# Gate logits of a graph-network stage as row sums on VectorE instead of narrow matmuls on TensorE

## The chip, the cores and the metric

The kernel runs on one core of a Trainium2 chip. The metric is the device time of one execution in microseconds (us), lower is better. Engines are called PE (TensorE matmul; PEld is its weight load), DVE (VectorE), ACT (ScalarE), POOL (GpSimd) and SP (SyncE, here a queue that issues DMAs). Lines such as L1123 are lines of the kernel before.

## The reference

A graph has 10000 nodes with 512 features (D) and 160000 edges, sorted by their target `dst`. Two layers follow each other. The first is a mixture of four experts of two graph convolutions each, the second a graph transformer. What the change touches is the first layer:

```
def gnn_layer(x, gate_W, gate_b, Wl, bl, Wr, edge_index):
    gates = softmax(x @ gate_W + gate_b)             # 10000 x 4
    top_v, top_i = top_k(gates, 2)
    inv_deg = 1 / max(deg, 1)  (0 where deg is 0)
    for e in range(4):                               # the experts
        h = x
        for l in range(2):
            aggr = segment_sum(h[src], dst) * inv_deg
            h = relu(aggr @ Wl[e, l] + bl[e, l] + h @ Wr[e, l])
    out = the two chosen experts' h, weighted by top_v, summed
x = layernorm(x + gnn_layer(x, ...))
...
x = layernorm(x + transformer_layer(x, ...))
```

The gate logits are the product `x @ gate_W`, with gate_W of 512 x 4, plus a bias of four numbers.

## The kernel before

The nodes are cut into 79 blocks of 128. The first stage (about the first 4.2 ms) computes the first convolution of all four experts, the second the second convolution, and the last the transformer layer. The change touches only the first stage.

**The first stage** goes over 40 superblocks of two blocks (the first one has a single block). For a block, the features of the edges' sources are fetched by indirect DMAs of POOL (`pull`, L1059) into a ring of ten tiles and summed by target with one-hot matmuls (`p_ag`, L1084); the one-hot tile `oh` and its sums `slots` are made on DVE (L891, L1070), and a small matmul with ones (L1092) gives the degree, from which DVE makes `inv_deg` (L1095). ACT scales the sum to `ag`. `turned_all` transposes `ag` and the block's own rows `xb` on PE (L1107) and ACT copies both into one tile `tt`. The gate logits are then matmuls of `tt`'s transposed `xb` (four weights of 128x128 per block) by `gw`, of 4 columns (L1182), and DVE adds the bias into `gate_w` (L1184). `conv` for one expert is 64 matmuls of 128x128 by 128x256 and ReLU on ACT (L1123, L1125); `products` multiplies the result by the second layer's Wl (L1133), copies to `y` and stores `y_tab` and `h_tab` by SP's queue.

The gather of the next superblock is cut in five pieces, called drives here (each two rounds of four matmuls per block column, 16 records on PE), and they are put between the other work. The order on PE per superblock is: drive 1, gates, conv 0, drive 2, conv 1, drive 3, prod 0, conv 2, drive 4, prod 1, conv 3, drive 5, prod 2, transposes of the next superblock, prod 3. The order on PE, DVE, ACT and POOL is the order in which the program is written (a manual schedule); SP's order is set by a scheduler.

**Work alongside.** Between the parts of `conv` the function `side` issues steps of another job, the ordering of the edges by source for the transformer layer. Until about 1.45 ms these are steps of `plan_src` on DVE: 158 counts (L913, four per call of `side`), then prefix sums in which PE multiplies by the tile `upper` (L930, L937; `upper` is made by an iota on POOL and a comparison on DVE, L927), then 158 scans of three instructions (L947, L950, L951). After that, `side` issues `scatter_src`: seven indirect DMAs of POOL (L993) per `conv`.

**Scratch.** The plan's tiles `m`, `num_i`, `dig_i`, `upper` and `part` are tiles of their own, and `h` has four buffers, one for each expert.

Of the kernel before, what the change touches and what calls it, by code (L numbers as in the profile page):

```python
# [8 lines left out]
F32 = mybir.dt.float32  # L9
BF16 = mybir.dt.bfloat16  # L10
I32 = mybir.dt.int32
U8 = mybir.dt.uint8
AF = mybir.ActivationFunctionType
ALU = mybir.AluOpType
# [616 lines left out]
def fast(ctx: ExitStack, tc: tile.TileContext, a: dict, out: bass.AP, bad: bass.AP):  # L631
# [240 lines left out]
    for e in range(NE):  # L872
        load_to(wl[e], a["L0_gnn_Wl"][e, 0])
        load_to(wr[e], a["L0_gnn_Wr"][e, 0], nc.scalar)
    gw = load_w(wp, "gw", a["L0_gnn_gate_W"], KD, NE)
    gb = wp.tile([P, NE], F32, name="gb")
    nc.sync.dma_start(gb, rows_bcast(a["L0_gnn_gate_b"], NE))
    bl = wp.tile([P, NE, KD], F32, name="bl")
# [17 lines left out]
    DIG = 1024.0  # L896
    SC = max(C, 2 * D)

    def plan_src(pool, ps):
        src_i = pool.tile([P, SC], I32, name="scan")[:, :C]  # L900
        nc.sync.dma_start(src_i, a["src"].rearrange("(p c) -> p c", c=C))
        pair = pool.tile([P, SC], BF16, name="pair")[:, :C]
        digit = pool.tile([P, C], BF16, name="digit")
        nc.vector.tensor_single_scalar(addr_i, src_i, 6, op=ALU.logical_shift_right)
        nc.vector.tensor_copy(pair, addr_i)
        nc.vector.tensor_scalar(addr_i, src_i, 5, 1, op0=ALU.logical_shift_right,
                                op1=ALU.bitwise_and)
        nc.vector.tensor_scalar(digit, addr_i, DIG - 1.0, 1.0, op0=ALU.mult, op1=ALU.add)
        yield
        count = pool.tile([P, NPR], F32, name="count")  # L910
        for b in range(NPR):
            m = pool.tile([P, C], BF16, name="m")
            nc.vector.scalar_tensor_tensor(m, pair, float(b), digit, op0=ALU.is_equal,  # L913
                                           op1=ALU.mult, accum_out=count[:, b:b + 1])
            yield
        num_i = pool.tile([P, NPR], I32, name="num_i")
        dig_i = pool.tile([P, NPR], I32, name="dig_i")
        nc.vector.tensor_copy(num_i, count)
        num = pool.tile([P, NPR, 2], F32, name="num")
        nc.vector.tensor_single_scalar(dig_i, num_i, 1023, op=ALU.bitwise_and)  # L920
        nc.vector.tensor_copy(num[:, :, 0], dig_i)
        nc.vector.tensor_single_scalar(dig_i, num_i, 10, op=ALU.logical_shift_right)
        nc.vector.tensor_copy(num[:, :, 1], dig_i)
        upper = pool.tile([P, P], F32, name="upper")
        nc.gpsimd.iota(upper, pattern=[[1, P]], base=0, channel_multiplier=-1,
                       allow_small_or_imprecise_dtypes=True)
        nc.vector.tensor_scalar(upper, upper, 0.0, None, op0=ALU.is_gt)  # L927
        flat = num.rearrange("p b q -> p (b q)")
        total = ps.tile([P, 512], F32, name="mm")
        nc.tensor.matmul(total[:, :NW], ones, flat, start=True, stop=True)  # L930
        top = pool.tile([P, 2], F32, name="top")
        nc.vector.tensor_reduce(top[:, 0:1], total[:, :NW], axis=AX.X, op=ALU.max)
        nc.vector.tensor_reduce(top[:, 1:2], total[:, :NW], axis=AX.X, op=ALU.add)
        nc.vector.tensor_scalar(fail[:, 1:2], top[:, 0:1], float(SL), None, op0=ALU.is_gt)
        nc.vector.tensor_scalar(fail[:, 2:3], top[:, 1:2], float(E), None, op0=ALU.not_equal)
        first = ps.tile([P, 512], F32, name="mm")
        nc.tensor.matmul(first[:, :NW], upper, flat, start=True, stop=True)  # L937
        two = first[:, :NW].rearrange("p (b q) -> p b q", q=2)
        nc.vector.tensor_copy(num, two)
        nc.vector.scalar_tensor_tensor(count, num[:, :, 1], DIG, num[:, :, 0],  # L940
                                       op0=ALU.mult, op1=ALU.add)
        nc.vector.memset(addr, 0.0)
        yield
        one = ones[:, 0:1].to_broadcast([P, C])
        for b in range(NPR):
            m = pool.tile([P, C], BF16, name="m")
            nc.vector.scalar_tensor_tensor(m, pair, float(b), digit, op0=ALU.is_equal,  # L947
                                           op1=ALU.mult)
            s = pool.tile([P, SC], F32, name="scan")[:, :C]
            nc.vector.tensor_tensor_scan(s, one, m, count[:, b:b + 1], op0=ALU.mult, op1=ALU.add)  # L950
            nc.vector.copy_predicated(addr, m.bitcast(mybir.dt.int16), s)  # L951
            yield

        nc.vector.tensor_sub(addr, addr, digit)
        rank = pool.tile([P, SC], I32, name="scan")[:, :C]
        nc.vector.tensor_copy(rank, addr)
        nc.vector.tensor_scalar(digit, digit, 1.0, 10.0 / (DIG - 1.0), op0=ALU.subtract,
                                op1=ALU.mult)
        nc.vector.tensor_copy(addr_i, digit)
        nc.vector.tensor_tensor(rank, rank, addr_i, op=ALU.logical_shift_right)  # L960
        yield
        nc.vector.tensor_scalar(digit, digit, 0.1, None, op0=ALU.mult)
        nc.vector.scalar_tensor_tensor(addr, pair, 2.0, digit, op0=ALU.mult, op1=ALU.add)
        nc.vector.tensor_scalar(addr, addr, float(CAP), None, op0=ALU.mult)
        part = pool.tile([P, C], I32, name="part")
        nc.vector.tensor_scalar(part, rank, 7, 7, op0=ALU.logical_shift_right,
                                op1=ALU.bitwise_and)
        nc.vector.tensor_add(addr, addr, part)
        nc.vector.tensor_single_scalar(part, rank, P - 1, op=ALU.bitwise_and)
        nc.vector.scalar_tensor_tensor(addr_i, part, float(NC), addr, op0=ALU.mult, op1=ALU.add)  # L970
        yield
# [75 lines left out]
    with p1, tc.tile_pool(name="p1k", bufs=1) as kp, tc.tile_pool(name="p1", bufs=2) as dp, \  # L1047
# [62 lines left out]
        def turned_all(rows):  # L1110
            tt = dp.tile([P, 2, KD, 2 * P], F32, name="tt", bufs=1)
            for i, (b, xb, ag) in enumerate(rows):
                turned(ag, tt[:, 0, :, i * P:(i + 1) * P])
                turned(xb, tt[:, 1, :, i * P:(i + 1) * P])
            return tt

        def conv(tt, e, n):
            h = dp.tile([P, KD, 2 * P], F32, name="h", bufs=4)
            for f in range(KD):
                ph = pm.tile([P, D], F32, name="mm")  # L1120
                for i, w in enumerate((wl[e], wr[e])):
# [17 lines left out]
            nc.sync.dma_start(h_tab[s, :, e, :, :n], h[:, :, :n])  # L1139

        fill = fill_slots()
        plan = plan_src(kp, pm)
        scat = scatter_src(mp)
        planned, planning = [], [0]

# [19 lines left out]
        with tc.manual_schedule(engines={ET.PE, ET.DVE, ET.Activation, ET.Pool}):  # L1165
# [7 lines left out]
            for s in range(NSB):  # L1173
# [2 lines left out]
                more = gather(s + 1, ahead) if s + 1 < NSB else iter(())  # L1176

                drive(more, 1)
                for i, (b, xb, ag) in enumerate(rows):
                    pg = psm.tile([P, NE], F32, name="small")  # L1180
                    for k in range(KD):
                        nc.tensor.matmul(pg, tt[:, 1, k, i * P:(i + 1) * P], gw[:, k, :],  # L1182
                                         start=(k == 0), stop=(k == KD - 1))
                    nc.vector.tensor_add(gate_w[:, b, :], pg, gb)  # L1184
                h = []
                for e in range(NE):
                    h.append(conv(tt, e, n))
# [614 lines left out]
```

## Time and profile before

| What | Value |
|---|---|
| Time before, median of 4 runs | 11294.47 us (11210.12 to 11340.56) |
| Profiled execution, own time | 11198.82 us |
| Its span | 11197.0 us |
| Mean granted clock of PE | 0.957 |
| First stage | to about 4200 us |
| PE, DVE, ACT, POOL busy | 9895.5, 5398.5, 2941.7, 7054.4 us |
| Largest group on PE | conv, L1123: 8960 matmuls, 2003.4 us |

Times are in microseconds, and mean durations of one instruction in nanoseconds. A line of the groups reads: line, engine, operation, output and inputs, shapes, number; then busy time and mean of one; then the idle time of the engine just before them, and what ended it. "issue" is idle time in which no wait is seen. A matmul of f32 appears as two records (two passes), so 16 records in a line are 8 matmuls.

### The profile page before, as it was taken

The page shows a single profiled execution, that of the slowest core. Times are in us where ns is not written, and L with a number is a line of the kernel's source. Part 1 is how long each engine was busy: PE and PEld are TensorE (multiplying, and loading weights), DVE is VectorE, ACT ScalarE, POOL GpSimd, SP SyncE. Part 2 cuts the span into 40 slices and gives each one's busy share as a digit, 9 for nine tenths or more (in the row PEclk, how much of TensorE's full clock was granted, in tenths as well). Part 3 has the DMA queues.
Part 4 walks back from the last instruction along what each step waited for, and adds up shares of the span by engine and source line. Part 5 has one row for each costly group of instructions (what it writes and reads, how often), then busy time and mean ns, then how long its engine had stood idle before and what let it go on. Part 6 is the DMA issues. An engine that isn't in the chain of part 4 may idle for free.

```text
span 11197.0 us, 169204 instructions
## 1 busy us (share of the span) xinstructions
PE 9895.5 (88%) x63887; PEld 5680.3 (51%) x63887; DVE 5398.5 (48%) x8205; ACT 2941.7 (26%) x5390; POOL 7054.4 (63%) x6972
## 2 busy tenths in 40 slices
PE   7999999999999988888888989888788888888887
PEld 4666666656666654333333333333555555555554
DVE  6888930000000022333333333334888888788886
ACT  1111111111111111111111111111455555555554
POOL 5566666666666655665666656665666666666664
PEclk8999999999999989999999999998899999999999
DMA  6554554444444436777777777776777777777774
GB/s 200 180 158 154 157 159 145 144 133 144 147 145 150 149 96 232 239 263 237 252 244 261 251 233 262 247 244 212 231 226 235 226 227 235 221 227 226 226 223 129
DMA packets 1110443, 2258.69 MB, mean 202 GB/s; under 512 B 284587, under 2 KB 534342, under 8 KB 1108848
## 3 DMA queue, kind: packets, MB, share of 16 engines
q0 software_dynamic: 622352, 1654.70, 46.4%
q1 hardware_dynamic: 479546, 579.42, 15.7%
q10 hardware_dynamic: 7718, 13.65, 0.4%
q8 instruction: 507, 8.31, 0.3%
q14 instruction: 320, 2.62, 0.1%
HBM read 2300.44 MB, written 380.18 MB: 239 GB/s over the span
## 4 chain that ended last, share of the span: by engine, by line
PE 70%; DVE 10%; ACT 7%; issue 7%; another core or an unknown queue 4%; DMA 1%; POOL 0%; SPq 0%; ACTq 0%; DVEq 0%; POOLq 0%
PE mm L1123 18%; PE mm L1133 9%; PE mm L1314 8%; PE mm L1276 7%; PE p_ag L1353 6%; PE p_ag L1084 4%; PE bank L1542 3%; PE sums L1632 3%; PE bank L1551 3%; PE bank L1502 2%; DVE m L913 2%; PE qe L1690 2%; DVE s L1731 2%; ACT L1544 2%
## 5 line engine op out<-in xcount | busy, mean ns | idle before, releaser
L1059 POOL DMA_INDIRECT ring<-in_x_dram,idx_t x1580 | 1917.2, 1213 | 1240.9 <-PE p_ag L1084 719.8
L1123 PE MATMUL mm<-tt,big 128*128 128x256 f32 (+1 forms) x8960 | 2003.4, 381 | 41.6 <-issue 39.9
L1123 PEld LDWEIGHTS mm<-tt,big 128*128 128x128 f32 x8960 | 1696.9, 192 | 360.4 <-issue 124.2
L993 POOL DMA_INDIRECT sorted<-pay,addr x1250 | 1263.2, 1011 | 385.5 <-issue 364.8
L1476 POOL DMA_INDIRECT kv<-kv_all,meta x1185 | 1284.6, 1084 | 332.3 <-issue 227.2
L1314 PE MATMUL mm<-big,hb 128*128 128x512 f32 x2528 | 1210.5, 613 | 102.2 <-issue 94.3
L1259 POOL DMA_INDIRECT y<-y_tab,ix x920 | 935.3, 1017 | 478.6 <-issue 216.9
L1276 PE MATMUL mm<-big,z_t 128*128 128x512 f32 x1896 | 923.4, 625 | 262.5 <-DVE t L1321 209.8
L1133 PE MATMUL mm<-wn,h 128*128 128x512 f32 x2528 | 1128.5, 599 | 1.6 <-issue 1.4
L1259 POOL DMA_INDIRECT ring<-y_tab,ix x660 | 679.2, 1029 | 637.2 <-PE p_ag L1353 365.0
L891 DVE TENSOR_TENSOR oh<-loc_t,iota_w 128x640 f32<-128x640 bf16 x158 | 130.8, 829 | 1780.0 <-remote 652.4
L1125 ACT ACTIVATE h<-mm,bl 128x256 f32<-128x256 f32 (+1 forms) x640 | 297.1, 471 | 2533.6 <-PE mm L1123 1356.2
L1542 PE MATMUL bank<-big,big 128*128 128x256 f32 (+1 forms) x2560 | 673.1, 406 | 221.4 <-ACT big L1544 212.8
L1314 PEld LDWEIGHTS mm<-big,hb 128*128 128x128 f32 x2528 | 480.4, 195 | 734.5 <-issue 687.0
L1704 DVE TENSOR_TENSOR kv<-qe,kv 128x1024 f32<-128x1024 f32 x711 | 729.4, 1040 | 159.1 <-PE qe L1690 158.2
L1133 PEld LDWEIGHTS mm<-wn,h 128*128 128x128 f32 x2528 | 469.0, 191 | 602.2 <-issue 581.3
L1618 POOL TENSOR_TENSOR ohp<-oh,p 128x512 f32<-128x512 bf16 x316 | 331.1, 1048 | 688.5 <-ACT p L1609 687.0
L1276 PEld LDWEIGHTS mm<-big,z_t 128*128 128x128 f32 x1896 | 374.2, 200 | 752.5 <-issue 502.1
L1377 ACT ACTIVATE t<-t,gsel 128x512 f32<-128x512 f32 x158 | 109.2, 723 | 2328.4 <-DVE t L1375 1552.4
L1542 PEld LDWEIGHTS bank<-big,big 128*128 128x128 f32 x2560 | 496.7, 203 | 384.5 <-ACT big L1544 272.0
L1731 DVE TENSOR_REDUCE s<-kv 128x40 f32<-128x2560 f32 x237 | 663.8, 2801 | 0.0
L1551 PE MATMUL bank<-big,big 128*128 128x512 f32 x1264 | 595.4, 597 | 57.0 <-ACT big L1544 56.2
(251 smaller groups left out, 14138.4 us busy)
## 6 DMA issues: line engine op xcount, KB each, us to landing
y_tab<-y SPq DMA_DIRECT2D x632, 256.0 KB
hb<-h_tab SPq DMA_DIRECT2D x316, 256.0 KB
h_tab<-h SPq DMA_DIRECT2D x156, 512.0 KB
kv_all<-kvt SPq DMA_DIRECT2D x79, 516.0 KB
xb<-in_x_dram SPq DMA_DIRECT2D x156, 256.0 KB
q_all<-q SPq DMA_DIRECT2D x79, 384.0 KB
q<-q_all SPq DMA_DIRECT2D x237, 128.0 KB
ring<-in_x_dram,idx_t POOLq DMA_INDIRECT x1580
```

The lines of the kernel that those rows point to most:

```text
L993: inst = nc.gpsimd.indirect_dma_start(out=sorted1[:], out_offset=bass.IndirectOffsetOnAxis(ap=addr_i[:, c0 + c:c0 + c + 1], axis=0), in_=p ...
L1059: nc.gpsimd.indirect_dma_start(out=gbuf[i % GB], out_offset=None, in_=x, in_offset=bass.IndirectOffsetOnAxis(ap=window(idx_t, b)[:, j, c:c ...
L1123: nc.tensor.matmul(ph[:, :n], w[:, k, f * P:(f + 1) * P], tt[:, i, k, :n], start=(i + k == 0), stop=(i == 1 and k == KD - 1))
L1133: nc.tensor.matmul(py, h[:, k, i * P:(i + 1) * P], wn[e][:, k, :], start=(k == 0), stop=(k == KD - 1))
L1259: nc.gpsimd.indirect_dma_start(out=ybuf[i % YB], out_offset=None, in_=y_flat, in_offset=bass.IndirectOffsetOnAxis(ap=ahead[b][1][:, j, c:c ...
L1276: nc.tensor.matmul(po, z_t[:, k, :], wqkv[i][:, k, :], start=(k == 0), stop=False)
L1314: nc.tensor.matmul(pr, hb[:, k, :], wr[e][:, k, :], start=(k == 0), stop=False)
L1476: nc.gpsimd.indirect_dma_start(out=kvb[w % KB][:, c, :], out_offset=None, in_=kv_all[:], in_offset=bass.IndirectOffsetOnAxis(ap=blocks[b][ ...
L1542: nc.tensor.matmul(ph, up(f, k), z_t[:, k, :m], start=(k == 0), stop=(k == KD - 1))
L1551: nc.tensor.matmul(po, hid[:, k, i * P:(i + 1) * P], w2[k // KD][:, k % KD, :], start=(k == 0), stop=False)
L1704: nc.vector.tensor_tensor(k, qe.pop((w, g))[:, :len(cs), :], k, op=ALU.mult)
L1731: nc.vector.tensor_reduce(s, kv[:, :, :D].rearrange("p c (h d) -> p c h d", h=H), axis=AX.X, op=ALU.add)
```

## The change

The matmuls of L1182 and the add from PSUM go. In `turned_all`, after a block's transposes, DVE multiplies the block's untransposed rows `xb` by one column of the gate weights, four times, and the instruction's accumulator gives the row sum directly to `gate_w`; a fifth instruction adds the bias. The gate weights are for that laid on all 128 partitions as a tile of 512 x 4 (8 KB per partition), with the four experts side by side, so that one expert's column has a stride of 16 bytes. The products themselves are written to a tile that nobody reads (`unread`, bf16).

To make room, `h` has three buffers instead of four, and one tile `part` is shared by `m`, `num_i`, `dig_i`, `upper`, `part` and `unread`.

```diff
-    gw = load_w(wp, "gw", a["L0_gnn_gate_W"], KD, NE)
+    gw = wp.tile([P, D, NE], F32, name="gw")
+    gate_wt = a["L0_gnn_gate_W"]
+    nc.sync.dma_start(gw, bass.AP(tensor=gate_wt.tensor, offset=gate_wt.offset,
+                                  ap=[[0, P], [1, D * NE]]))
...
-    def plan_src(pool, ps):
+    def plan_src(pool, ps, part):
...
-            m = pool.tile([P, C], BF16, name="m")
+            m = part.bitcast(BF16)[:, :C]
...
-        num_i = pool.tile([P, NPR], I32, name="num_i")
-        dig_i = pool.tile([P, NPR], I32, name="dig_i")
+        num_i, dig_i = part[:, P:P + NPR], part[:, P + NPR:P + 2 * NPR]
...
-        upper = pool.tile([P, P], F32, name="upper")
+        upper = part.bitcast(F32)[:, :P]
...
-        part = pool.tile([P, C], I32, name="part")
+        part = part[:, :C]
...
             for i, (b, xb, ag) in enumerate(rows):
                 turned(ag, tt[:, 0, :, i * P:(i + 1) * P])
                 turned(xb, tt[:, 1, :, i * P:(i + 1) * P])
+                for e in range(NE):
+                    nc.vector.scalar_tensor_tensor(unread, xb, 1.0, gw[:, :, e], op0=ALU.mult,
+                                                   op1=ALU.mult, accum_out=gate_w[:, b, e:e + 1])
+                nc.vector.tensor_add(gate_w[:, b, :], gate_w[:, b, :], gb)
             return tt
 
         def conv(tt, e, n):
-            h = dp.tile([P, KD, 2 * P], F32, name="h", bufs=4)
+            h = dp.tile([P, KD, 2 * P], F32, name="h", bufs=3)
...
-        plan = plan_src(kp, pm)
+        part = kp.tile([P, SC], I32, name="part")
+        unread = part.bitcast(BF16)[:, SC:SC + D]
+        plan = plan_src(kp, pm, part)
...
                 drive(more, 1)
-                for i, (b, xb, ag) in enumerate(rows):
-                    pg = psm.tile([P, NE], F32, name="small")
-                    for k in range(KD):
-                        nc.tensor.matmul(pg, tt[:, 1, k, i * P:(i + 1) * P], gw[:, k, :],
-                                         start=(k == 0), stop=(k == KD - 1))
-                    nc.vector.tensor_add(gate_w[:, b, :], pg, gb)
                 h = []
```

More of the change, by code (lines that the diff above doesn't have):

```diff
@@ L945, in plan_src @@
         for b in range(NPR):
-            m = pool.tile([P, C], BF16, name="m")
+            m = part.bitcast(BF16)[:, :C]
             nc.vector.scalar_tensor_tensor(m, pair, float(b), digit, op0=ALU.is_equal,
```

## The prediction

> **What bounds the kernel now.** I read the 40 slices of the span first, because the diff touches one stage only, and then the chain that ended last.
>
> ```profile
> PE   7999999999999988888888989888788888888887
> DVE  6888930000000022333333333334888888788886
> ...
> PE 70%; DVE 10%; ACT 7%; issue 7%; another core or an unknown queue 4%; DMA 1%; POOL 0%; SPq 0%; ACTq 0%; DVEq 0%; POOLq 0%
> ```
>
> Each digit stands for 280 us. The first stage fills the first fifteen. In slices 2 to 5 both engines are nearly full: DVE works off the plan of the sorted edges (counts L913, then scans L947 to L951). From slice 6 to 14 DVE has almost nothing to do and PE still shows 9. So moving work from PE to DVE meets a full engine first and an empty one later. The view by windows gives the two parts in numbers (columns: stretch, length, then busy time of PE, PEld, DVE, ACT, POOL, the granted clock, DMA share, GB/s).
>
> ```profile
> 398.00:1469.00 1071.00, 1071.00 (x4805) 731.00 (x4797) 961.31 (x633) 172.05 (x331) 720.10 (x441) 1.00 0.50 157
> 1567.00:4042.00 2475.00, 2376.72 (x10028) 1559.62 (x10028) 156.36 (x372) 354.59 (x691) 1605.50 (x1684) 0.98 0.47 145
> ```
>
> In the first stretch PE is busy all the time, 97.2 us per superblock of two blocks (eleven in 1071 us), and DVE 961 / 11 = 87.4 us of them. In the second a superblock takes mostly 105.0 us and 107.6 in the mean (23 in 2475 us), although PE has the same work: some 8 us go to stalls. The PE timeline of one superblock shows the larger one (start, length, instruction, number; in brackets idle time and its releaser), and POOL's timeline stands beneath it.
>
> ```profile
> 1775.19 1.92 PE L1084 MATMUL p_ag<-ring,oh 128*32 128x512 f32 x16
> 1777.05 1.95 PE L1182 MATMUL small<-gw,tt 128*128 128x4 f32 x16
> 1778.85 14.06 PE L1123 MATMUL mm<-tt,big 128*128 128x256 f32 x64
> 1792.84 1.06 PE L1084 MATMUL p_ag<-ring,oh 128*32 128x512 f32 x6
> 1794.22 1.02 PE L1084 MATMUL p_ag<-ring,oh 128*32 128x512 f32 x2 [0.31 <-issue]
> 1796.33 0.16 PE L1092 MATMUL small<-ones,slots 128*128 128x1 f32 x1 [0.90 <-issue]
> ```
> ```profile
> 1786.96 1.04 POOL L993 DMA_INDIRECT sorted<-pay,addr  x1 [0.30 <-issue]
> ...
> 1794.77 0.98 POOL L993 DMA_INDIRECT sorted<-pay,addr  x1 [0.30 <-issue]
> ```
>
> The same 18 records that take 2.3 us in an early superblock (302.32 to 304.63) run here from 1792.84 to 1798.77, 5.9 us, with no semaphore named. That happens while, and until about 3 us after, POOL's seven scatters (L993) run: 1786.96 to 1795.75. I went through the five drives (the quarter-size steps of the gather) of all late superblocks: of the 26 that start up to 5.7 us after such a scatter run began, 25 are not stalled; of those starting at 5.9 us or later nearly all are. Drive 2 always starts at 5.9: 1792.84 − 1786.96.
>
> **The removed part.** The gate matmuls are one row between drive 1 and conv 0.
>
> ```profile
> L1182 PE MATMUL small<-gw,tt 128*128 128x4 f32 x632 | 76.9, 254 | 0.0
> L1182 PEld LDWEIGHTS small<-gw,tt 128*128 128x128 f32 x632 | 73.6, 191 | 33.2 <-issue 33.2
> L1184 DVE TENSOR_TENSOR gate_w<-small,gb 128x4 f32<-128x4 f32 x79 | 12.4, 162 | 569.4 <-PE p_ag L1084 400.7 <-PE small L1182 130.4 <-remote 22.0
> ```
>
> Their busy times overlap with each other, so the price is read from the timeline: conv 0 starts 1778.85 − 1777.05 = 1.80 us after the gates do, for 16 pairs. Where PE has no stall that is the gain of a superblock. The whole would be 79 blocks × 0.9 = 71 us.
>
> **The added part.** Per block DVE gets four row sums of 128x512, four accumulator reads and an add. The bare product of two f32 tiles and the read of an accumulator are in the trace; one operand with a stride of 16 bytes isn't, in this length.
>
> ```profile
> L913 DVE SCALAR_TENSOR_TENSOR m<-pair,digit 128x1250 bf16<-128x1250 bf16 x158 | 230.8, 1461 | 5.2
> L913 DVE DVE_READ_ACCUMULATOR m<-pair,digit 128x1 f32 x158 | 13.1, 83 | 0.0
> L1291 DVE SCALAR_TENSOR_TENSOR left<-mm,q 128x512 f32<-128x512 f32 x79 | 54.7, 692 | 149.3 <-ACT q L1290 142.1 <-ACT z L744 7.1
> L1070 DVE TENSOR_REDUCE slots<-oh 128x128 f32<-128x640 f32 x79 | 99.4, 1258 | 2.7
> L854 DVE TENSOR_REDUCE none<-out_w 128x1 f32<-128x640 f32 x3 | 2.4, 799 | 0.0
> L1029 DVE TENSOR_TENSOR c<-gate_w 128x26 f32<-128x26 f32 x24 | 5.0, 210 | 0.8
> L1029 DVE TENSOR_TENSOR c<-gate_w 128x2 f32<-128x2 f32 x12 | 1.9, 161 | 0.4
> ```
>
> Low end: 0.69 us, L1291, no penalty for the stride. High end: L1029 reads both operands at a stride of 16 bytes and pays (210 − 161) / 24 = 2.0 ns per element; 0.157 + 512 × 2.0 gives 1.18 us. Between them, L1070 against L854 shows 0.72 ns per element more for a strided read of one operand, 0.69 + 0.37 = 1.06. I take 1.06, the row with one strided operand. A block then costs 4 × (1.06 + 0.083 + 0.045 spacing) + 0.16 = 4.9 us, bounds 3.4 and 5.4; a superblock 9.8 us less the two old adds of 0.16, so 9.5, bounds 6.5 and 10.5.
>
> [...]
>
> **Stage by stage.** *Start.* The gate weights come as 128 rows of 8 KB, 1 MB, instead of 512 pieces of 16 bytes, on SP's queue ahead of gb, bl and wn. The first gate add and the first ReLU wait for gb and bl, which land at 115.3 us; at the 223 GB/s of the first 200 us a megabyte is 4.7 us, and the small pieces fall away: −2 to +5, I take +2.
>
> *Counts.* Until 357 us DVE is the late engine. PE waits for it at the prefix sums of the plan:
>
> ```profile
> 369.09 1.39 PE L930 MATMUL mm<-num,ones 128*128 128x316 f32 x2 [11.60 <-DVE upper L927]
> ```
>
> Row sums of block 0 fall into DVE's idle 92 to 115 us; those of about four later blocks lie ahead of the counts, and 4 × 3.4 to 4 × 4.9 is 14 to 20 us; PE's earlier arrival is eaten by the same wait. I take +16. The iota of upper now waits for DVE's counts, since it writes the shared tile; queued behind it are pulls, which PE needs only after the same wait, so nothing is added; without that cover it would be one refill of the ring, 8 pulls × 1.3 = 10 us, once.
>
> *Scans*, about 12 superblocks. PE loses 1.80 of 97.2 us and leaves 95.4. DVE needs 87.4 + 9.5 = 96.9, bounds 93.9 and 97.9. It can hide some of that in its idle place:
>
> ```profile
> 886.92 0.16 DVE L1184 TENSOR_TENSOR gate_w<-small,gb 128x4 f32<-128x4 f32 x1 [8.04 <-issue]
> ```
>
> These 8.04 us and 1.23 after them were waits for the gate matmuls, and DVE is no longer held there. DVE may fall 1.5 us behind per superblock at 96.9, 18 over twelve; what is late then is the scale of ag (inv_deg L1095), whose reader needs it about 14 to 20 us after it is ready now. So PE keeps its gain, −1.8 × 12 = −22; at the high price 2.5 × 12 = 30 less 14 of slack is lost again, bound +8 with the pulls, which take 1.2 to 2.5 us instead of 1.0 while DVE is full (L1059 at 891 us: 2.48).
>
> [...]
>
> *Afterwards*, 25 superblocks with DVE at 156 us in 2475. The row sums are hidden in its idle time, even at the high price. PE reaches drive 2 1.8 us earlier, at 4.1 us into the scatter run instead of 5.9. Plainly that is −1.8 × 25 = −45. If the end of the stall is fixed by POOL, whose run starts after the pulls of drive 1, nothing is left: 0. If drive 2 escapes the stall, 5.9 turns to 2.4 and a superblock gains 1.8 + 3.7 = 5.5. Two late superblocks had an unstalled drive 2 by chance and were no shorter: 112.6 us (at 2197.8) and 106.5 (at 2539.7), with the pause in conv 2 or drive 3 instead. So I take about −50, the plain gain and a few escapes.
>
> *Nothing.* Three h buffers for four: the nearest reuse is 49 us after the store was issued. The loads of xb now wait on SP for DVE as well, with the y_tab stores of prod 3 and the h_tab store behind them; y is reused some 30 us later, more than DVE's lag. If that cover went, a store of 256 KB late by 5 us would delay prod 0 by it.
>
> **Sum.** +2 + 16 − 22 − 50 = −54 us. The profiled execution took 11198.8 us, span 11197.0, and lies at the lower end of the four runs (11210 to 11341, median 11294.5); I apply the difference to the median: 11240 us.
>
> **Rivals.** *A, the forecast:* within 1%, 11190 to 11330. PE's plain gain, partly spent on DVE's backlog of the counts. *B, drive 2 escapes:* the 25 of 26 rule speaks for it, the two superblocks above against. 23 × 5.5 = 127 instead of 50: 11294 − 4 − 127 = 11163; with drive 5's stall gone too (9.6 each, 221) 11069. *C, slower:* POOL's scatter run and the pulls behind it come earlier relative to PE, drive 2 passes, and the pause lands in a convolution as at 2197.8, 112.6 instead of 105.0 us: 23 × 7.6 = 175 more, 11294 − 4 + 175 = 11465. It decides from about 16 of the 23 superblocks on, 11294 − 4 + 122 = 11412. For it speaks that seven late superblocks already take 106 to 117 us; against it that they are seven of 23. *D, no gain at all:* the stall's end is pinned to POOL and nothing moves: +2 + 16 − 22 + 0, 11290; it lies within A's range.
>
> **How the numbers follow.** A and D together 0.55, B 0.25, C 0.20. The time is that of A, 11240. The range reaches over B's plain size and C's lower part, 11080 to 11390. A measurement of this kernel can tell about 1% (113 us) from no change: faster 0.25, same 0.55, slower 0.20.
>
> **What would show it.** Right: conv 0 starts directly after drive 1; the row sums near 1.06 us; PE's wait at the prefix sums about 28 us instead of 11.6; scan superblocks of 95.4 us with PE full; late superblocks near 103 us. Wrong: row sums above 1.18 us, or PE waiting for inv_deg in the scans (DVE bounds); late superblocks at 105 (D), below 101 (B) or above 108 (C); a change in the stages from 4.2 ms on, which I take to be untouched.

## The result, and the profile after

The kernel after takes 11295.5 us (median of 44 runs), the kernel before 11257.0 us (median of 70 runs beside them): ratio 1.0041, 95% interval 1.0027 to 1.0056. The forecast was 11240 us, half a per cent faster; the change costs a little instead. The profiled execution of after took 11263.6 us, its span is 11261.8 us. It lies 32 us below its kernel's median, and that of before 58 us below, so the two traces stand 64.8 us apart and the medians 38.5: what the traces give for a stage is somewhat more than a typical pair of executions would.

One thing has to be known for all numbers that follow. The stalls of PE beside POOL's scatters, which both of these profiles show, were there in some measuring sessions and wholly absent in others: the kernel before took 11257, 11118, 11108 and 11128 us in sessions with them and 10226, 10217 and 10217 us in sessions without, and one chip showed both. Kernels are compared within a session only, and each result below says "with stalls" or "without".

The 40 slices of the span after show where the first stage changed: DVE now has something to do in slices 6 to 14. PE's row is the same as before over the first fifteen slices; tenths are too coarse for what follows.

```profile
PE   7999999999999988889988888888788888888887
...
DVE  7999941111111132333333333333878878878886
```

The groups of the first stage give the price of the new work, and the PE timeline gives the one wait that was forecast to grow (start, length, instruction; in brackets the idle time before it and its releaser). The 64 matmuls given above for one `conv`, and the 8960 of L1123, are records, so half as many matmuls.

```profile
L1118 DVE SCALAR_TENSOR_TENSOR part<-xb,gw 128x512 bf16<-128x512 f32 x316 | 345.6, 1094 | 8.1
```
```profile
367.24 1.39 PE L932 MATMUL mm<-num,ones 128*128 128x316 f32 x2 [26.79 <-DVE part L929]
```

A row sum takes 1094 ns (1.06 us was forecast), and PE's wait at the prefix sums grew from 11.6 to 26.8 us (28 was forecast). The windows of the two parts of the stage come next; the second runs from the transposes that open superblock 15 to those that open superblock 38, 23 superblocks, as in all windows below.

```profile
398.00:1469.00 1071.00, 1068.75 (x4706) 724.99 (x4705) 1049.93 (x802) 172.71 (x335) 745.46 (x449) 1.00 0.51 158
1544.60:4094.20 2549.60, 2348.08 (x9662) 1521.55 (x9661) 343.75 (x719) 357.99 (x693) 1657.03 (x1690) 0.96 0.45 141
```

In the scan part PE is still full, and a superblock takes 95.4 us instead of 97.2, as forecast. In the late part one takes 2549.6 / 23 = 110.9 us; the same 23 take 2475.5 us in the trace of before (1556.5 to 4032.0), 107.6 each. The balance, read from where each superblock's transposes start on PE (before and after):

| Mark | Before | After | Difference |
|---|---|---|---|
| Superblock 3 | 388.1 | 385.6 | -2.5 |
| Superblock 13 | 1361.2 | 1339.6 | -21.6 |
| Superblock 15 | 1556.5 | 1544.6 | -11.9 |
| Superblock 38 | 4032.0 | 4094.2 | +62.2 |
| End of the span | 11197.0 | 11261.8 | +64.8 |

So all of the loss, and more, comes from 23 superblocks in which DVE is nearly idle; from 4.1 ms on nothing changed. Counted over the places where PE's next matmul starts more than 0.6 us after the one before, with 0.2 us taken off each, PE loses 308 us in this stretch instead of 166. These are called lost time below.

What such a superblock looks like in after: DVE's row sums, POOL, and PE, in their timelines.

```profile
1961.76 1.08 DVE L1118 SCALAR_TENSOR_TENSOR part<-xb,gw 128x512 bf16<-128x512 f32 x1
...
1965.20 1.09 DVE L1118 SCALAR_TENSOR_TENSOR part<-xb,gw 128x512 bf16<-128x512 f32 x1
```
```profile
1961.27 1.04 POOL L1061 DMA_INDIRECT ring<-in_x_dram,idx_t  x1 [2.19 <-remote]
...
1965.34 1.83 POOL L1061 DMA_INDIRECT ring<-in_x_dram,idx_t  x1 [0.30 <-issue]
...
1968.78 1.87 POOL L1061 DMA_INDIRECT ring<-in_x_dram,idx_t  x1 [0.30 <-issue]
...
1972.26 1.00 POOL L1061 DMA_INDIRECT ring<-in_x_dram,idx_t  x1 [0.31 <-issue]
1973.56 1.04 POOL L995 DMA_INDIRECT sorted<-pay,addr  x1 [0.30 <-issue]
...
1981.91 0.99 POOL L995 DMA_INDIRECT sorted<-pay,addr  x1 [0.28 <-POOL pay L993]
1983.20 1.04 POOL L1061 DMA_INDIRECT ring<-in_x_dram,idx_t  x1 [0.30 <-issue]
```
```profile
1988.44 0.60 PE L1109 MATMUL mm<-ident,xb 128*128 128x128 f32 x4
1990.09 0.66 PE L1109 MATMUL mm<-ident,ag 128*128 128x128 f32 x4 [1.05 <-ACT y L1142]
1995.06 1.12 PE L1109 MATMUL mm<-ident,xb 128*128 128x128 f32 x4 [4.31 <-issue]
1995.97 5.58 PE L1139 MATMUL mm<-wn,h 128*128 128x512 f32 x10
```

Two pulls beside the row sums take 1.83 and 1.87 us instead of 1.00, so the eight of them last from 1961.27 to 1973.26, 12.0 us. The seven scatters follow, and the next pulls start 0.30 us behind the last scatter, without any pause. Seven and a half microseconds after the first of these pulls, at 1990.75, PE stands for 4.31 us within the transposes for no cause that the profile names, and the matmuls after them crawl.

The crawl has a cause that the trace does show, the clock granted to PE. It is 1.00 while PE stands (1990.75 to 1994.80), and 0.50 from 1994.80 to 1998.22; in that stretch the matmuls of L1139 start every 0.85 us, after it every 0.43. Over the 23 superblocks the clock is halved 28 times in after, 218 us in all, and 14 times in before, 99 us; each time PE had stood for at least 1.4 us in all within the 7 us before. So such a stall is paid for twice, by the time in which PE stands and by the half speed after it. If PE worked through all of these stretches, half speed cost some 109 us in after and 50 in before (an upper estimate, half of 218 and of 99).

### The profile page after: what moved, and what is told of

Same layout as the page of the kernel before. It is cut to its first block, busy times and chain, and to the rows that moved or that the text cites. A ratio compares the mean times of both kernels' runs of the same rounds, so it can differ in the third digit from the quotient of the medians.

```text
span 11261.8 us, 168599 instructions
## 1 busy us (share of the span) xinstructions
PE 9855.3 (88%) x63255; PEld 5609.9 (50%) x63255; DVE 5738.4 (51%) x8837; ACT 2938.5 (26%) x5390; POOL 7115.9 (63%) x6972
## 4 chain that ended last, share of the span: by engine, by line
PE 60%; DVE 19%; issue 8%; ACT 7%; another core or an unknown queue 4%; DMA 1%; POOL 1%; ACTq 0%; SPq 0%; POOLq 0%; DVEq 0%
PE mm L1129 13%; PE mm L1316 8%; PE mm L1278 7%; PE mm L1139 7%; PE p_ag L1355 6%; DVE scan L952 3%; PE bank L1544 3%; PE sums L1634 3%; PE bank L1553 3%; PE bank L1504 2%; PE p_ag L1086 2%; DVE part L916 2%; DVE addr L953 2%; PE qe L1692 2%
## 5 line engine op out<-in xcount | busy, mean ns | idle before, releaser
L1061 POOL DMA_INDIRECT ring<-in_x_dram,idx_t x1580 | 1962.9, 1242 | 1163.5 <-PE p_ag L1086 615.6
L1129 PE MATMUL mm<-tt,big 128*128 128x256 f32 (+1 forms) x8960 | 2050.2, 384 | 105.1 <-issue 100.1
L1139 PE MATMUL mm<-wn,h 128*128 128x512 f32 x2528 | 1149.2, 605 | 22.1 <-issue 16.5
L1139 PEld LDWEIGHTS mm<-wn,h 128*128 128x128 f32 x2528 | 474.5, 193 | 640.1 <-issue 625.6
```

The source lines that it names most:

```text
L1061: nc.gpsimd.indirect_dma_start(out=gbuf[i % GB], out_offset=None, in_=x, in_offset=bass.IndirectOffsetOnAxis(ap=window(idx_t, b)[:, j, c:c ...
L1129: nc.tensor.matmul(ph[:, :n], w[:, k, f * P:(f + 1) * P], tt[:, i, k, :n], start=(i + k == 0), stop=(i == 1 and k == KD - 1))
L1139: nc.tensor.matmul(py, h[:, k, i * P:(i + 1) * P], wn[e][:, k, :], start=(k == 0), stop=(k == KD - 1))
```

## The experiments

Seven theories were put to the test. T1: the loss comes from PE's earlier arrival (the removed matmuls moved the drives against the scatters). T2: it comes from the row sums on DVE. T6 and T7 split T2: through POOL, held back by the second SBUF operand, or through DVE's time as such. T3 says that the sign hangs on whether the stalls are there, T4 blames the scratch tiles, T5 the width of the scattered rows. All ratios are against the kernel before in the same session, with a 95% interval. The times of late superblocks are of one profiled execution each, and stand beside each other across sessions; only after_again, cheap_after and bal_after, and no_gate_2, both_2, share_only and wide_after, share a session with stalls. In the table "late" is the mean of the 23 superblocks, "direct" the number of the 92 runs of seven scatters whose next pulls follow within 0.6 us.

| Kernel | Stalls | Ratio | Late, us | Pull beside DVE's work, elsewhere, us | Direct |
|---|---|---|---|---|---|
| before (profile above) | with | 1 | 107.6 | -, 1.02 | 9 |
| after (profile above) | with | 1.0041 (1.0027 to 1.0056) | 110.9 | 1.32, 1.02 | 24 |
| after_again | with | 1.0057 (1.0034 to 1.0080) | 110.5 | 1.32, 1.02 | 20 |
| both_2 | with | 1.0044 (1.0023 to 1.0065) | 110.2 | 1.33, 1.02 | 20 |
| no_gate_2 | with | 0.9946 (0.9928 to 0.9965) | 106.8 | -, 1.02 | 6 |
| share_only | with | 0.9996 (0.9976 to 1.0016) | 106.5 | -, 1.02 | 4 |
| one_input_3 | with | 0.9995 (0.9968 to 1.0023) | 106.8 | 1.01, 1.03 | 6 |
| cheap_after | with | 0.9975 (0.9956 to 0.9995) | 106.5 | 1.19, 1.02 | 12 |
| wide_after | with | 1.0036 (1.0017 to 1.0056) | 108.8 | 1.35, 1.02 | 14 |
| bal_after | with | 1.0062 (1.0038 to 1.0086) | 109.3 | 1.37, 1.03 | 20 of 115 |
| after_3 | without | 0.9954 (0.9937 to 0.9970) | 96.1 | 1.53, 1.00 | 90 |
| both | without | 0.9996 (0.9986 to 1.0005) | 97.3 | 1.47, 1.01 | 91 |
| no_gate | without | 0.9914 (0.9898 to 0.9931) | 95.4 | -, 1.01 | 92 |
| one_input, one_input_2 | without | 0.9948, 0.9934 | 95.4, 95.5 | 1.01, 1.01 | 92, 92 |
| cheap_2 | without | 0.9925 (0.9909 to 0.9942) | 95.5 | 1.21, 1.00 | 92 |

### Each half of the change alone: both, no_gate

Row sums with the matmuls kept and their result unread (both):

```diff
                 drive(more, 1)
+                for i, (b, xb, ag) in enumerate(rows):
+                    pg = psm.tile([P, NE], F32, name="small")
+                    for k in range(KD):
+                        nc.tensor.matmul(pg, tt[:, 1, k, i * P:(i + 1) * P], gw[:, k, :],
+                                         start=(k == 0), stop=(k == KD - 1))
                 h = []
```

The kernel before without them (no_gate; four features of a node stand for its logits, which it leaves out):

```diff
-                    pg = psm.tile([P, NE], F32, name="small")
-                    for k in range(KD):
-                        nc.tensor.matmul(...)
-                    nc.vector.tensor_add(gate_w[:, b, :], pg, gb)
+                    nc.vector.tensor_add(gate_w[:, b, :], xb[:, :NE], gb)
```

> The kernel after, with the 316 gate matmuls kept on TensorE in their old place and their result unread, so that PE comes to drive 2 at its old phase while VectorE still makes the row sums. Theory T1 (what was lost after the plan comes from PE's timing against POOL's scatter runs): late superblocks (1567 to 4042 us) go back from the 110.9 us of the kernel after to about 107.6, lost issue time of PE there from 287 to about 166 us, and the whole is the kernel before plus the wait at the prefix sums and the start, +10 to +25 us, ratio 1.001 to 1.002. Rival T2 (the row sums themselves disturb POOL or PE there): late superblocks stay at 110 or more, the whole is +60 to +90 us, ratio 1.006 or more.

> The kernel before with the gate matmuls left out and nothing in their place: the first four features of a node stand for its logits, so the gate logits are left out of the computation. PE gets its earlier phase, VectorE gets no row sums. T1: scan superblocks 95.4 us, and late ones near 111 as in the kernel after; -3.6 - 22 + 75 = about +45 us on the kernel before, ratio 1.003 to 1.005. T2: the removed matmuls are simply gained, late superblocks 103 to 105.8, about -70 us, ratio 0.994.

These first runs met a session without stalls, in which neither theory had anything to explain: PE is full through the late superblocks (95.4 us each in no_gate, 97.3 in both), no_gate gains 0.86%, both stands at the kernel before. They were repeated.

> The kernel before with the gate matmuls left out and nothing in their place (four features of the node stand for its logits, so the gate logits are left out of the computation), again, to have it in a run in which POOL's scatters stall PE: the first time no stalls were there, and 316 removed groups gained 88 us. T1 (PE's phase): late superblocks near 110 us as in the kernel after, the whole +30 to +60 us, ratio 1.003 to 1.005. T2 (the row sums on VectorE cost what was lost): late superblocks 103 to 106, the whole -60 to -90 us, ratio 0.992 to 0.995.

> Row sums on VectorE and the unread gate matmuls on PE together, again. T1: PE's phase is that of the kernel before, late superblocks near 107.6 us, the whole +10 to +25 us. T2: late superblocks 110 us or more and the whole +60 to +90 us, ratio 1.006 or more.

With stalls the two answers are clear, and against T1. Windows of the 23 late superblocks, first no_gate_2, then both_2 (length, then busy time of PE, PEld, DVE, ACT, POOL, clock, DMA share, GB/s):

```profile
1523.50:3979.00 2455.50, 2333.53 (x9662) 1514.45 (x9661) 144.60 (x357) 356.09 (x691) 1603.53 (x1682) 0.99 0.47 146
```
```profile
1564.90:4099.20 2534.30, 2372.53 (x10030) 1560.99 (x10029) 343.26 (x717) 353.10 (x690) 1644.36 (x1683) 0.97 0.45 141
```

PE's earlier arrival alone (no_gate_2) costs nothing late: 106.8 us. The row sums with PE's old timing (both_2) cost nearly the whole of it: 110.2 us, and POOL's busy time grows by 41 us with the same work. T1 fell; of T2, the late superblocks came as expected, while the ratio of both_2, 1.0044, stayed below its 1.006. The pair says a second thing: against share_only of the same session, whose gate matmuls are in place and whose late superblocks take 106.5 us, taking the matmuls away gains nothing late. PE's 1.8 us vanish into the stalls, as rival D of the prediction had it.

### The scratch alone: share_only

The kernel before with three h buffers and the tile `part` shared.

> The kernel before with the shared scratch tile and three h buffers alone, gates still by TensorE. T1 and T2: nothing, within 5 us of the kernel before (iota of upper waits for the counts, under PE's own wait of 11.6 us at the prefix sums). Rival T4 (the three h buffers hold a conv back until a store has read its h): late superblocks longer, +40 us or more.

```profile
1560.60:4011.10 2450.50, 2364.51 (x10030) 1549.94 (x10029) 148.59 (x359) 353.53 (x691) 1603.32 (x1682) 1.00 0.47 146
```

Ratio 0.9996 and late superblocks of 106.5 us: T4 fell, and the prediction's "Nothing" held. This kernel and both_2, of the same session, differ in the row sums and the loading of their weights: 84 us in the 23 superblocks by the traces, 70 us by the medians of the whole (11172.3 and 11102.3). The clock is halved for 24 us in share_only and for 140 us in both_2, which by the estimate above is up to 58 of the 84 us.

### One SBUF operand instead of two: one_input

The kernel without gate matmuls, and where the row sums were, reductions of the same length over one operand:

```diff
+                for e in range(NE):
+                    nc.vector.tensor_reduce(unread[:, e:e + 1], wn_cols, axis=AX.X, op=ALU.add)
+                nc.vector.tensor_add(gate_w[:, b, :], xb[:, :NE], gb)
```

> The kernel before without gate matmuls, and in the place of the row sums eight reductions per superblock of 128x960 f32 on VectorE, each about as long as a row sum (1.09 us by 2801 ns for 2560 elements) but with one operand from SBUF instead of two (four features of the node stand for its logits, so the gate logits are left out). T6 (a row sum's second SBUF operand holds POOL's pulls back): pulls beside them stay near 1.02 us instead of 1.32, late superblocks as in the kernel without gates (106.8 us) and not 110.5, the whole as that kernel plus about 20 us for the prefix sums, ratio 0.994 to 0.998. Rival T7 (it is VectorE's time, whatever it reads): late superblocks 110 us, ratio 1.003 or more.

> The reductions with one SBUF operand in the place of the row sums (logits left out), again, beside the kernel after. Without stalls as in its first run, 0.995. With stalls, T6 (the second operand holds POOL's pulls, and that sets the stalls off): late superblocks near 106.8 us and ratio 0.995 to 0.998. T7 (VectorE's time as such): late superblocks near 110 us, ratio 1.003 or more.

> The reductions with one SBUF operand a third time, only to meet executions with stalls. With stalls, T6: pulls beside the reductions near 1.02 us, late superblocks near 106.8 us, ratio 0.995 to 0.998. T7: late superblocks near 110 us, ratio 1.003 or more. Without stalls: 0.993 to 0.995 again, and the question stays open.

The first two met sessions without stalls (0.9948, interval 0.9931 to 0.9964, and 0.9934, 0.9918 to 0.9951); what they showed is that pulls beside the reductions take 1.01 us where pulls beside row sums take 1.47 or 1.53. The third had stalls. Its group and its window:

```profile
L1117 DVE TENSOR_REDUCE unread<-wn 128x1 f32<-128x960 f32 x316 | 340.9, 1143 | 0.0
```
```profile
1555.80:4011.80 2456.00, 2319.49 (x9662) 1503.18 (x9661) 333.53 (x533) 355.73 (x691) 1605.89 (x1682) 0.99 0.46 146
```

DVE is as busy as in both_2 (334 against 343 us) but POOL is not (1606 against 1644), and a late superblock takes 106.8 us, just as with no DVE work at all. T7 fell in the place where the loss was, with one reserve: of one_input_3's session there is a trace of this kernel alone, so 106.8 is held against 110.2 to 110.9 of the kernels with full row sums in three other sessions (bal_after: 109.3, wide_after: 108.8), and against 106.5 to 107.6 of those without DVE work. The ratio of the whole, 0.9995, lies a little above T6's range: this kernel is already 32 us behind no_gate_2 at superblock 15 (1555.8 against 1523.5), where 20 were allowed for the counts, and another 36 us come behind superblock 38, in stages that the edit doesn't touch. POOL's timeline of one_input_3 shows the place that was shown of after:

```profile
2058.61 1.05 POOL L1060 DMA_INDIRECT ring<-in_x_dram,idx_t  x1 [1.86 <-remote]
...
2067.81 1.00 POOL L1060 DMA_INDIRECT ring<-in_x_dram,idx_t  x1 [0.30 <-issue]
2069.11 1.04 POOL L994 DMA_INDIRECT sorted<-pay,addr  x1 [0.30 <-issue]
...
2076.93 0.98 POOL L994 DMA_INDIRECT sorted<-pay,addr  x1 [0.30 <-issue]
2080.64 1.05 POOL L1060 DMA_INDIRECT ring<-in_x_dram,idx_t  x1 [2.73 <-PE p_ag L1085]
```

Eight pulls last 10.2 us, the scatters are done at 2077.91, and the next pull then waits 2.73 us for PE. Of no_gate_2 it is the same, 2.70 us:

```profile
2131.76 1.04 POOL L1059 DMA_INDIRECT ring<-in_x_dram,idx_t  x1 [1.80 <-remote]
...
2150.08 0.98 POOL L993 DMA_INDIRECT sorted<-pay,addr  x1 [0.30 <-issue]
2153.76 1.05 POOL L1059 DMA_INDIRECT ring<-in_x_dram,idx_t  x1 [2.70 <-PE p_ag L1084]
```

That pause is what the row sums take away: POOL comes 1.8 us later, PE's drive has freed the ring by then, and the pulls follow the scatters directly. Over the late part of the two first traces, the lost time in the 16 us from the start of such direct pulls is 6.5 us in the mean (after, 24 times) or 5.1 us (before, 9 times), and 0.6 or 0.1 us where there was a pause. That the direct pulls cause the stalls is likely from this; no run here took them away alone.

### A shorter row sum: cheap

The gate weights copied once by ScalarE, so that one expert's 512 weights lie side by side:

```diff
-    gw = wp.tile([P, D, NE], F32, name="gw")
+    gw = wp.tile([P, NE, D], F32, name="gw")
...
+    for e in range(NE):
+        nc.scalar.copy(gw[:, e, :], gw_in[:, :, e])
...
-                    nc.vector.scalar_tensor_tensor(unread, xb, 1.0, gw[:, :, e], ...)
+                    nc.vector.scalar_tensor_tensor(unread, xb, 1.0, gw[:, e, :], ...)
```

> The kernel after, with the gate weights copied once by ScalarE so that each expert's column lies contiguous; the row sums then read no stride. The step of the prediction on the stride: 1094 ns falls to 690 to 745 ns, a superblock's row sums from 9.6 to about 6.5 us, PE's wait at the prefix sums from 26.8 to about 21 us, scan and late superblocks unchanged because DVE's time is hidden there. The whole 5 to 10 us under the kernel after. Rival: the price is not the stride (the two f32 operands or the accumulator), and the row sum stays near 1.09 us.

> The row sums from contiguous gate weights again, beside the one-operand kernel on the same chip. T6: a shorter row sum holds pulls back less (1.19 us beside it instead of 1.32), late superblocks near 106.5 us, ratio 0.996 to 0.999 as in its first run (0.9975).

```profile
L1121 DVE SCALAR_TENSOR_TENSOR part<-xb,gw 128x512 bf16<-128x512 f32 x316 | 218.2, 690 | 8.4
```
```profile
1531.50:3981.90 2450.40, 2316.23 (x9661) 1510.02 (x9660) 267.82 (x717) 357.18 (x691) 1624.37 (x1683) 0.98 0.47 146
```

The row sum falls to 690 ns, the price of the row with contiguous operands in the prediction; the stride cost 0.40 us of 1.09, 0.79 ns per element. The expectation of 5 to 10 us was far too small: the medians of cheap_after and after_again, in one session, are 11106.6 and 11187.6 us, 81 apart. Of the 103 us by which their traces stand apart at superblock 38 (3981.9 against 4085.1), 91 arise in the late part (2541.7 against 2450.4 us for 23 superblocks). The effect of a held pull is not in proportion to its length; the clock is halved for 79 us of the late part here and for 174 us in after_again. This kernel is faster than the kernel before in both kinds of session, by 0.25% with stalls and 0.75% without. It is faster than after in the session with stalls that they share; without stalls their ratios, 0.9925 and 0.9954, come from two sessions and the intervals overlap.

### Scatters moved, spread or widened

Without scatters in the first stage (`side` returns at once when the plan is done), made from before and from after:

> The kernel before, with the scatters of the first stage moved behind the second stage (all 697 that do not fit into the second stage run at its end, about 697 x 1.29 = 900 us). T1: late superblocks without stalls, 97.2 us as in the plan phase, lost issue time of PE near 0; the whole about 11257 + 900 - 23 x 10.4 = 11920. The rival that stalls come with the pulls alone: late superblocks stay above 102.

> The kernel after with the same move of the scatters. T1: late superblocks 95.4 us, and the kernel is faster than its counterpart made from the kernel before, by 22 + 23 x 1.8 less 18 for start and prefix sums, about 45 to 50 us. T2 (row sums disturb): late superblocks above 97 us and no gain, or a loss, against the counterpart.

Both met a session without stalls: 11130.6 and 11058.9 us, late superblocks of 97.2 and 95.4 us, so the kernel with row sums is 72 us faster here by the medians. The two traces stand 49 us apart at superblock 38 (3777.5 and 3728.3), as the expectation had it. That the scatters set the stalls off could not be seen in them.

The 28 scatters of a superblock spread as 4, 4, 8, 8 and 4:

```diff
-                drive(scat, 2 if f < KD - 1 else 1)
+                drive(scat, 1 if e < 2 else 2)
...
                     tt = turned_all(ahead)
+                if planned:
+                    drive(scat, 4)
```

> The kernel after, with the 28 scatters of a superblock spread anew: 4, 4, 8, 8 in the four convolutions and 4 before the last products, instead of 7 in each convolution, so that POOL's pulls plus scatters between two drives are shorter than PE's work between them. T1: where stalls are there, POOL never runs pulls directly behind scatters, the stalls of 5 to 13 us go, late superblocks 96 to 101 us, the whole 150 to 300 us under the kernel after. Where no stalls are there, no change against the kernel after. Rival (each scatter stalls PE by itself, 25 us per hundred): late superblocks as in the kernel after.

It met stalls: late superblocks 109.3 us, ratio as after_again. POOL's runs still end where PE is ahead (20 of 115 are direct), and the 150 to 300 us were not there. Rows of 64 bytes (`WP = 16` instead of 10):

> The kernel after with rows of 64 bytes instead of 40 for the scattered edges (the 24 added bytes are zero and unread), to see what of the scatters stalls PE. T5 (rows that fill only part of a 64-byte piece of memory, or lie across two, hold the memory up): late superblocks without stalls, 95.4 to 98 us, 200 to 300 us less in the first stage. Rival (the number of scattered rows, or POOL's queue, not their width): stalls as in the kernel after, and slightly more time in the last stage, which reads 1.6 times as many bytes of edges.

Late superblocks 108.8 us, and PE's lost time is still 253 us (318 in after_again): T5 fell, and its piece of 64 bytes was a guess of the author's that no trace shows. Three scatters behind each four pulls, instead of seven in a row:

> The kernel before with three scatters behind each four pulls on POOL instead of seven in a row behind eight pulls: the same number, finer mixed. If PE's stalls come from long runs of scatters: late superblocks fall from 106.5 towards 97 to 102 us, up to 200 us gained. Rival (they come from POOL's sum of pulls and scatters, which stays): late superblocks 105 to 108 us, no gain.

> The same mix of scatters, with the row sums on VectorE from contiguous gate weights: a try at a kernel that beats both. If the finer mix removes the stalls: late superblocks about 95.4 to 100 us and ratio 0.975 to 0.99. If not, as the kernel with contiguous weights, 0.997.

Both met a session without stalls, so that what they were made for stays untried. There the mix costs: 1.0017 (1.0007 to 1.0027) and 0.9988 (0.9978 to 0.9998), against 0.9925 for the same row sums without it, and late superblocks take 98.1 and 98.8 us.

### The kernel after in both kinds of session

> The kernel after, unchanged. In the first four runs the kernel before took 10226 us instead of 11257, and no superblock showed the stalls during POOL's scatters. Theory T3 (the sign hangs on whether the scatters stall PE in that execution): where late superblocks show no stalls, all forty keep the gain of 1.8 us, less about 18 for the prefix sums and the start: 10226 - 55 = 10170, ratio 0.993 to 0.996; where the stalls are there again, ratio 1.002 to 1.006. Rival T2 (the row sums cost by themselves): no faster than before in either state, ratio 1.000 or more.

> The kernel after, unchanged, a third time. T3 (the sign hangs on whether PE is stalled during POOL's scatters in these executions): with stalls (the kernel before near 11100 us or more) ratio 1.003 to 1.007; without them (the kernel before near 10220 us) all superblocks at 95.4 us and ratio 0.993 to 0.996, since POOL then has slack for pulls of 1.3 to 1.5 us. Rival (row sums cost in both): ratio 1.000 or more without stalls too.

T3 held: 1.0057 with stalls, 0.9954 without. The window of after_3:

```profile
1546.00:3757.10 2211.10, 2209.44 (x9662) 1491.27 (x9661) 344.19 (x717) 358.79 (x691) 1652.43 (x1687) 1.00 0.52 162
```

PE is full, and POOL is busy 1652 of 2211 us with pulls as late as anywhere (1.53 us beside row sums): here the held pulls left PE busy for 2209 of 2211 us, while beside stalls, at 1.32 us a pull, PE's lost time in after was 308 us against 166 in before.

## Why the prediction was wrong, step by step

- *Price of a row sum*: 1.06 us taken, 1.094 measured; it was right that the stride costs, and about by the row with one strided operand. The row of the low end, L1291, reads a PSUM tile and a bf16 one by the kernel's lines and not two f32 tiles of SBUF; that two such tiles side by side take the same 690 ns was shown only by cheap_after.
- *Start*: +2 taken; the first transposes come at 94.2 instead of 91.9 us.
- *Counts*: the wait at the prefix sums was right (28 forecast, 26.8), the +16 was not: the prefix sums start at 367.24 instead of 369.09 us. The step added the row sums to DVE's work and left the start of the counts where it was. But the old gate add of the first block (L1184) stood ahead of the counts on DVE, and DVE was idle for 22.02 us before it, until 115.29 (by the prediction's reading it waited for `gb`); in after the add of that block runs at 88.53 without a wait, and the first count starts at 98.86 instead of 118.79. These 19.9 us pay for the row sums: superblock 1 became 19.5 us shorter, superblock 2, with the longer wait, 19.9 us longer, and the last count ends at 365.70 instead of 367.44. Start and counts together gave -2.5 where +18 was forecast. That is luck of these executions in part: where there were no stalls, two kernels that are the kernel before up to there (no_scat_before, spread_before) come to the first gate add at 103.03 and 104.70 instead of 115.29, and to superblock 3 at 375.7 and 378.1 us, and after_3 and no_scat_after at 387.1 and 386.3, so that the two steps cost 8 to 11 us.
- *Scans*: right for ten superblocks. 95.4 us each, -19 us from superblock 3 to 13, with DVE at 1050 of 1071 us. Superblocks 13 and 14, where the first scatters run, gave 10 of it back.
- *Afterwards*: the step that failed, -50 forecast for 25 superblocks and +74 measured for 23 of them. It holds two errors. The plain gain of 1.8 us is not there when the stalls are (no_gate_2): the prediction had this as rival D and gave too little to it. And "the row sums are hidden in its idle time, even at the high price" looked at DVE alone; they are hidden there, and cost 3.7 us per superblock by the traces (both_2 less share_only, 110.2 - 106.5; 3.0 by the medians) through POOL. The prediction also had no term for the clock, which was halved for 218 us of this stretch instead of 99. The prediction had a row of it in hand, the pulls of up to 2.48 us in the plan part. It put the price on the plan part, where PE has slack for it, and none on the late part, where POOL's pulls and scatters fill most of the time.
- *The 25 of 26 rule* held for early drives (over the whole late part of before, 34 of the 35 that start within 5.75 us of a scatter run; in after 56 of 65) and not for late ones: in after the ten that start 5.9 to 8.9 us behind are all unstalled. Drive 2 does start 4.1 us into the run and passes, as forecast, and it was of no use: only 9 drives are stalled in after instead of 38, but the pause falls on whatever PE does then, as the superblocks at 2197.8 and 2539.7 us had shown.
- *Rival C* had the sign and, nearly, the place: pauses in convolutions and transposes. Its reason, PE's earlier arrival, is refuted by no_gate_2.
- *Nothing* (three h buffers, shared scratch) and the untouched later stages held.
- Without the stalls the plain terms held in sum: +2 + 16 - 22 - 45 = -49 forecast, and after_3 measured 0.0046 x 10217 = 47 us less by its ratio (40 by the medians). Two errors cancel there in part: start and counts 7 to 10 us too dear, and late superblocks at 96.1 instead of 95.4 us, 16 us over 23 of them.

In the late part a pull took 1.32 us in the mean beside row sums (after), 1.01 beside reductions of one operand (one_input_3) and 1.02 with no row sum beside it (before, and after). Operation, operand number and output were changed together in that test (a product with accumulator that writes 512 elements, against a reduction that writes one), so that it is the second operand which holds a pull is the author's guess and was not shown.

What stays open: why PE stands beside the scatters in some sessions and not in others (in before from 1793 to 1799 it does so at a granted clock of 1.00, so the clock isn't the first cause), and why pulls directly behind scatters prolong this. In those gaps the profile names no wait, and the DMA traffic is no sign either: 5 GB/s in that gap of before, 266 GB/s in the one of after at 1990.75.

## What to carry to other kernels

Idle time on the receiving engine isn't enough: list the engines that work beside the moved operation, and price what the operation does to their instructions, from rows where such pairs already overlap (here pulls of 1.2 to 2.5 us in the plan part against 1.0 elsewhere). Where a queue like POOL's lives from a pause of two microseconds, an operation's length can decide whether the pause survives; here 0.69 us mostly passed (12 of 92 runs direct) and 1.09 us did not (20 to 24). And a stall that the profile shows without a cause can take back a gain on the stalled engine in full (106.8 us late without the gate matmuls, no_gate_2, against 106.5 with them, share_only), so its share should be the first rival, with a weight.

## What was not expected of the hardware

- The same kernel took 10217 us and 11108 us on one chip in different sessions. In the first kind no late superblock of the kernels in the table had a stall, and the part behind superblock 38 took 6418 to 6437 us instead of 7054 to 7168.
- Pulls directly behind scatters are harmless to the kernels of the table in sessions without stalls (90 to 92 of 92 are direct there, and PE's lost time is at most 3.2 us in all; the finer mix, spread_cheap, has 44 us). In sessions with stalls the lost time behind them is 5 to 7 us each in the mean of most kernels, and 1.8 to 3.4 us in the three that have only four to six of them.
- A gap of PE can cost more than its own length: in after the granted clock fell to 0.50 behind 28 stalls, for 3.4 to 13.7 us each time.
- A 16-byte stride on one of two f32 operands of 512 elements costs 0.40 us (690 to 1094 ns).
